# A gated graph network: the turn of h between layers, by TensorE or by VectorE and an exchange through DRAM

## The chip, the cores and the metric

The kernel runs on one core of one Trainium2 chip. The metric is device time in microseconds (us) of one execution. The engines in the text: TensorE (PE; its weight loads are PEld), VectorE (DVE), ScalarE (ACT), GpSimd (POOL) and SyncE (SP), which here only issues DMAs. Every engine works through its own list of instructions in order and waits on semaphores where it needs another's result.

## The reference

There are 16 batches of 1024 nodes with 128 features. Layer 0 is a gated graph network of four steps behind a layer norm, layer 1 a graph convolution of four steps with a batch norm over all batches. Cut to what matters:

```python
h = relu(layernorm(x))                       # per batch: (1024, 128)
for i in range(4):                           # layer 0: GRU
    m = adj.T @ (h @ weight[i])              # adj: 1024 x 1024 of 0 and 1
    r = sigmoid(m @ w_ir + h @ w_hr + b)
    z = sigmoid(m @ w_iz + h @ w_hz + b)
    n = tanh(m @ w_in + b + r * (h @ w_hn + b))
    h = (1 - z) * n + z * h
x = x + h
h = relu(layernorm(x))
for i in range(4):                           # layer 1: conv
    h = relu(adj @ (h @ W[i]) + b[i])
    h = batchnorm over all batches and nodes
return x + h
```

## The kernel before

**Two parts.** The first part (`with ExitStack() as st`) runs layer 0 for the 16 batches, in pairs; it takes two thirds of the time. The second part runs the four convolutions over all batches, from a transposed copy of the adjacency that the first part has left in DRAM (`adjT_d`). A slower path for other inputs is not taken.

**How h lies.** The gates work on `hT`, features on partitions, 1024 nodes along the free axis, in two halves of 512. The aggregation `adj.T @ h` needs h with *nodes* on partitions, as the stationary operand. So h has to be turned once per layer. `features_times(None, ...)` (L491) does it: eight 128x128 transposes on TensorE into PSUM (L498, `hw_g<-ident,h`), then for each half a copy by ScalarE that rounds to the short float type (L502, `ghw`, the high part) and a subtraction by VectorE that keeps the rest (L503, the low part). High and low are multiplied with the adjacency one after the other (L525): 32 matmuls of 128x512 per layer and batch. The weight `weight[i]` is folded into the input weights (`w_mT`), so nothing stands between turn and aggregation.

**Two streams.** `sa` takes the even batches, `sb` the odd ones, half a layer apart. `half_step(one, two)` is the unit: `one` turns h and aggregates (`split_step`, `agg_step(0)`, `agg_step(1)`), `two` runs the gates of its layer for both halves (`gate_step(0)`, `gate_step(1)`: six fp32 matmuls each, L841; sigmoid of r L853, two VectorE operations L854 and L855, tanh L858, sigmoid of z L859, and the new h L864 to L866). On TensorE the order is turn, gates, aggregation. `agg_step` ends with two copies of PSUM by ScalarE (`m`, L816), which the next half-step's gates read. The first pair's opening runs under an order written out by hand for all engines; after it only POOL and SP keep the order of the code, and a scheduler places the instructions of TensorE, VectorE and ScalarE. `behind(x)` tells it to place the following instructions after `x` on their engine.

**Work beside it.** Around the change of batches the half-steps carry more. `fetch` loads four rows of blocks of the next adjacency into `stage`, `first_four` and `last_four` round them to `row` on POOL (L578), and `glance` reads their low half-words on ScalarE (L587, `junk`, which sets a flag for inexact inputs). `ahead` loads the next x (L540) and normalizes it (`prepare`: square root L628, eight L640). `finish` exchanges input and output across the turn: VectorE transposes 32x32 blocks (L677), SP stores them to DRAM (L591) and loads them back with the blocks permuted (L598, four loads for each half). `end_step` runs the stages of a finished batch: `arrive`, `tail_norm` (L696, statistics L624), and `rest` (norm, store). `transpose_on`, in the half-step in which a stream is at layer 1, casts all eight row blocks to bf16 on POOL (L609, `half`, two buffers), has SP turn each by a DMA transpose (L610), and stores the 2 MB tile (L916). That tile shares its buffer (`turned_tile`, one buffer) with `stage`.

**Queues.** SP issues the loads of the adjacency, the exchanges and the DMA transposes, in the order of the code; POOL issues the stores of x, y and adjT and the loads of x, between its casts.

Of the kernel before, what the change touches and what calls it, by code (L numbers as in the profile page):

```python
# [341 lines left out]
def exact_path(  # L342
# [39 lines left out]
    def tmp(name):  # L382
        return ps_t.tile([P, HALF], F32, tag="tmp", name=name)

    adjT_d = [dram.tile([P, NB, N], BF16, tag=f"adjT{b}", name=f"adjT_d{b}") for b in range(B)]
    xmid_d = [dram.tile([N, C], F32, tag=f"xmid{b}", name=f"xmid_d{b}") for b in range(B)]
    ymid_d = [dram.tile([P, N], F32, tag=f"ymid{b}", name=f"ymid_d{b}") for b in range(B)]

# [145 lines left out]
    with ExitStack() as st:  # L534
# [71 lines left out]
        def transpose_rows(b, row, j, adjT):  # L606

            t = work.tile([P, N], BF16, tag="half1", name=f"half{b}_{j}", bufs=2)
            nc.gpsimd.tensor_copy(t, row.bitcast(F32))  # L609
            nc.sync.dma_start_transpose(adjT[:, :, j * P : (j + 1) * P], t)  # L610

        def norm(xt, y, name):

# [57 lines left out]

        def blocks_out(src, name):

            ds = []
            for hf in range(NH):
                t = half_tile(f"t_{name}_{hf}").bitcast(F32)
                last = nc.vector.transpose(by_nodes(t), four_ways(src[:, hf * HALF : (hf + 1) * HALF]))  # L677
                ds.append(exchange_out(t, f"{name}_{hf}"))
            return ds, last

        def tail_norm(b, xt, hT, parts=None):

            for hf in range(NH):
                if parts:
                    pt = by_nodes(parts[hf])
                else:
                    pt = tmp(f"pt_x{b}_{hf}")
                    for q in range(BH):
                        k = hf * BH + q
                        nc.tensor.transpose(pt[:, q * P : (q + 1) * P], hT[:, k * P : (k + 1) * P], ident)  # L690
                    pt = four_ways(pt)
                for q in range(BH):
                    k = hf * BH + q
                    xk = xt[:, k, :].rearrange("p (a c) -> p a c", a=4)
                    mask = maskT[:, b * NB + k : b * NB + k + 1]
                    nc.vector.scalar_tensor_tensor(xk, pt[:, q, :, :], mask, xk, ALU.mult, ALU.add)  # L696
            nt = norm_stats(xt, f"mid{b}")
            if b + 1 < B:
                y = work.tile([P, N], F32, tag="h", name=f"y_mid{b}", bufs=7)
            else:  # L700
                y = xt.rearrange("p k c -> p (k c)")
            nc.gpsimd.dma_start(xmid_d[b].rearrange("(k p) c -> p k c", p=P), xt)

            def rest():
                norm_apply(xt, y, nt)
                nc.gpsimd.dma_start(ymid_d[b], y)

            return rest

# [9 lines left out]
        class Stream:  # L719


            def __init__(self, first):
                self.b, self.i, self.tag = first, 0, "AB"[first % 2]
                self.opened, self.across, self.ends, self.stage = None, False, [], None

            def open(self, xt):

# [25 lines left out]
            def normed(self, ks):  # L753
                norm_blocks(self.xt, self.y, self.norm, ks)

            def prepare(self):
                self.next_y = work.tile([P, N], F32, tag=f"y{self.tag}", name=f"y_in{self.b + 2}", bufs=1)
                norm_apply(self.next_x, self.next_y, self.next_norm)

            def fetch(self):  # L760

                if self.i == 3 and self.b + 2 < B:
                    stage = turned_tile(f"stage{self.b + 2}").bitcast(F32)
                    self.stage = [stage[:, 2 * q : 2 * q + 2, :].rearrange("p a n -> p (a n)") for q in range(4)]
                    stage_rows(self.b + 2, self.stage, range(4))

            def first_four(self):
                if self.stage:
# [5 lines left out]
            def last_four(self):  # L774
                if self.stage:
                    self.rows += round_rows(self.b + 2, self.stage, range(4, NB))
                    with behind(self.last_act):
                        glance(self.b + 2, self.stage, range(4, NB))
                    self.stage = None

            def take(self):
                self.xt, self.y = self.next_x, self.next_y
                self.across = True
                self.hT = work.tile([P, N], F32, tag="h", name=f"h_in{self.b}", bufs=7)
                return blocks_out(self.y, f"in{self.b}")[0]

            def split_step(self):
                nm = f"{self.b}_{self.i}"
                self.hw = hw_tiles(self.b, f"ghw{nm}")
                for g in range(NH):  # L790
                    if self.i > 0:
                        features_times(None, self.hT, self.hw, g, f"g{nm}")
                        continue
                    self.split_high(g)
                    self.split_low(g)
# [12 lines left out]
            def agg_rows(self, js):  # L808
# [3 lines left out]
                if js[-1] == NB - 1:  # L812
                    self.m = []
                    for hf in range(NH):
                        m = work.tile([P, HALF], F32, tag="m", name=f"m{self.b}_{self.i}_{hf}", bufs=4)
                        nc.scalar.copy(m, self.pm[hf])  # L816
                        self.m.append(m)

            def open_gates(self):
# [4 lines left out]
                hin = self.hT[:, :HALF]  # L824
                nc.tensor.matmul(self.opened[2], w_hhT[:, 0, 2 * C : 3 * C], hin, start=True, stop=True)

            def gate_step(self, hf, between=None):
                i, nm = self.i, f"{self.b}_{self.i}_{hf}"
                if hf == 0 and not self.opened:
                    self.new = work.tile([P, N], F32, tag="h", name=f"h{nm}", bufs=7)  # L830
# [21 lines left out]
                z = work.tile([P, HALF], F32, tag="z", name=f"z{nm}")  # L852
                self.first_act = nc.scalar.activation(r, pr, AF.Sigmoid, bias=brz[:, 3 * i : 3 * i + 1])  # L853
                nc.vector.scalar_tensor_tensor(r, phn, b_hn(i), r, ALU.add, ALU.mult)  # L854
                nc.vector.tensor_add(r, pxn, r)  # L855
                if between:
                    between()
                nc.scalar.activation(r, r, AF.Tanh, bias=b_in(i))  # L858
                self.last_act = nc.scalar.activation(z, pz, AF.Sigmoid, bias=brz[:, 3 * i + 1 : 3 * i + 2])  # L859
                ho = self.new[:, cols]  # L860
                if across:
                    nc.vector.tensor_sub(four_ways(ho), hin, four_ways(r))
                else:
                    nc.vector.tensor_sub(ho, hin, r)  # L864
                nc.vector.tensor_mul(ho, ho, z)  # L865
                self.last_dve = nc.vector.tensor_add(ho, ho, r)  # L866
                if hf == NH - 1:
# [3 lines left out]
            def ahead(self):  # L871

                if self.b + 2 >= B:
                    return
                if self.i == 2 and self is sa:
                    for stream in (sa, sb):
                        stream.next_x = load_x(stream.b + 2, nc.gpsimd)
                if self.i == 3:
                    with behind(self.last_act, self.last_dve):
                        self.prepare()  # L880

            def finish(self):

# [6 lines left out]
                    self.ends = [tail_norm(*args)]  # L890
                    return
                h_in = self.hT
                outs, last = blocks_out(args[-1], f"out{args[0]}")
                parts = [half_tile(f"n_{args[0]}_{hf}").bitcast(F32) for hf in range(NH)]

                def arrive():
                    for hf in range(NH):
                        exchange_in(ins[hf], h_in[:, hf * HALF : (hf + 1) * HALF])
                    for hf in range(NH):
                        exchange_in(outs[hf], parts[hf])  # L900
                    self.ends.append(lambda: self.ends.append(tail_norm(*args, parts)))

                self.ends = [arrive]

            def end_step(self, *after):
                if self.ends:
                    with behind(*after):
                        self.ends.pop(0)()

            def transpose_on(self):  # L910

                if self.i == 1:
                    adjT = turned_tile(f"adjT{self.b}")
                    for j in range(NB):
                        transpose_rows(self.b, self.rows[j], j, adjT)
                    nc.gpsimd.dma_start(adjT_d[self.b], adjT)  # L916

            def sums_ahead(self, two):

                if self.i == 2 and self.b + 2 < B:  # L920
                    self.next_norm = norm_tiles(f"in{self.b + 2}")
                    with behind(two.last_dve):
                        norm_sums(self.next_x, self.next_norm, range(NB))

        def half_step(one, two, gated=None, halfway=None):

            if one.i > 0:
                one.split_step()
            two.gate_step(0)
            two.first_four()  # L930
            two.gate_step(1)
            two.last_four()
            if gated:
                gated()
            if one.i == 0:
                one.split_step()
            one.agg_step(0)
            if halfway:
                halfway()
            one.end_step(two.last_act)  # L940
            two.end_step(two.last_dve)
            two.ahead()
            one.transpose_on()
            one.sums_ahead(two)
            one.agg_step(1)
            two.finish()
            one.fetch()
# [118 lines left out]
        with tc.manual_schedule(engines={mybir.EngineType.Pool, mybir.EngineType.SP}):  # L1066
            written[0] = False
            for s in range(2, B // 2 * L):
                half_step(sa, sb)
                half_step(sb, sa)  # L1070
            sb.gate_step(0)
            sb.gate_step(1)
            with tc.issue_after(sb.last_act.ins):
# [16 lines left out]
    def load_adjT(b, i):  # L1090
        ts = []
        block = None if b % 2 else turned_tile(f"block{b}_{i}")
        for j in range(NB):
            t = half_tile(f"packed{b}_{i}_{j}") if b % 2 else block[:, j, :]
            nc.sync.dma_start(t, adjT_d[b][:, j, :])
            r = row_tile(f"wide{b}_{i}_{j}")
            if j % 3 == 1:
                nc.scalar.copy(r, t)  # L1098
# [269 lines left out]
```

## Time and profile before

| what | value |
|---|---|
| median of 3 runs | 1826.63 us (1825.93 to 1826.99) |
| the profiled execution | 1827.16 us |
| its span, first to last instruction | 1825.0 us |
| granted TensorE clock, mean | 0.998 |
| busy: PE / DVE / ACT / POOL | 1800.1 / 1163.1 / 1139.4 / 364.1 us |
| turns on TensorE (L498, hw_g) | 384 transposes, 50.1 us busy |
| aggregation, first part (L525, pm) | 2048 matmuls, 504.5 us busy |
| casts to bf16 (L609) / DMA transposes (L610) | 128 / 128 |
| HBM read / written | 243.35 / 73.40 MB |

How to read the lines in this document: a group has line, engine, operation, output<-input by the program's names, partitions x elements, count | busy us, mean ns of one | idle time of its engine just before, and what ended it. Matmuls overlap, so the mean of one is longer than the distance to the next. A line of waits has who waited <- for whom: us in total, times, longest. A line of the chain or the timeline has start, length, what.

### The profile page before, as it was taken

How to read it: one execution, taken by the hardware profiler on the slowest of the kernel's cores; microseconds unless marked ns; L12 is line 12 of the kernel's file. 1: busy time of each engine (PE TensorE's matmuls, PEld its weight loads, DVE VectorE, ACT ScalarE, POOL GpSimd, SP SyncE). 2: the span in 40 equal slices, each digit the busy share in tenths (PEclk: the TensorE clock that was granted, in tenths of full speed). 3: DMA queues.
4: the chain of work that ended last, by engine and by line, in shares of the span. 5: the costliest groups of instructions: out<-in, count | busy, mean ns of one | idle time of the engine just before them, and what ended most of it. 6: DMA issues, size and time to landing. Idle time of an engine off the chain costs nothing.

```text
span 1825.0 us, 22200 instructions
## 1 busy us (share of the span) xinstructions
PE 1800.1 (99%) x7102; PEld 1228.8 (67%) x7102; DVE 1163.1 (64%) x2189; ACT 1139.4 (62%) x1773; POOL 364.1 (20%) x378
## 2 busy tenths in 40 slices
PE   8999999999999999999999999999999999999997
PEld 5565665666565656565656556667778888888886
DVE  7665755666656666666566565676666666667665
ACT  5448557557556655755754755467777768768764
POOL 3223223142232232222314213110100000000010
PEclk9999999999999999999999999999999999999999
DMA  7546475375464645647537557478966666667666
GB/s 249 132 129 198 101 202 193 107 165 186 152 167 145 218 125 164 215 91 208 188 105 160 205 167 189 134 250 309 309 215 228 234 230 232 231 230 237 236 231 243
DMA packets 293020, 351.88 MB, mean 193 GB/s; under 512 B 152620, under 2 KB 187216, under 8 KB 290848
## 3 DMA queue, kind: packets, MB, share of 16 engines
q1 hardware_dynamic: 278288, 275.33, 50.5%
q0 software_dynamic: 14080, 74.80, 11.8%
q8 instruction: 57, 0.93, 0.2%
q14 instruction: 67, 0.55, 0.1%
q10 hardware_dynamic: 528, 0.26, 0.0%
HBM read 243.35 MB, written 73.40 MB: 174 GB/s over the span
## 4 chain that ended last, share of the span: by engine, by line
PE 76%; ACT 9%; DMA 6%; DVE 5%; issue 2%; SPq 1%; POOL 0%; DVEq 0%; ACTq 0%; POOLq 0%
PE pm L525 17%; PE pc_m L525 12%; PE g_z L841 9%; PE g_r L841 8%; PE pc_g_r L525 6%; PE pc_g_z L525 6%; DMA stage<-in_adj_dram 5%; PE hw_c L500 4%; PE g_hn L841 4%; PE g_xn L841 4%; ACT junk L587 3%; PE hw_g L498 2%; ACT y_in L640 1%; DVE h L865 1%; ACT z L859 1%
## 5 line engine op out<-in xcount | busy, mean ns | idle before, releaser
L525 PE MATMUL pm<-row,ghw 128*128 128x512 f32 x2048 | 504.5, 403 | 0.4 <-POOL row L564 0.3
L525 PEld LDWEIGHTS pm<-row,ghw 128*128 128x128 f32 x2048 | 384.1, 188 | 108.7 <-issue 30.9
L525 PE MATMUL pc_m<-wide,chw 128*128 128x512 f32 x1024 | 246.0, 395 | 0.0
L525 PEld LDWEIGHTS pc_m<-wide,chw 128*128 128x128 f32 x1024 | 190.5, 188 | 42.2 <-issue 4.3
L858 ACT ACTIVATE r<-r,vecs 128x512 f32<-128x512 f32 x128 | 92.0, 719 | 181.8 <-DVE r L855 181.7
L525 PE MATMUL pc_g_r<-wide,chw 128*128 128x512 f32 x464 | 187.0, 403 | 0.3 <-ACT chw L502 0.3
L578 POOL CAST row<-stage 128x1024 fp32r<-128x1024 f32 x112 | 130.8, 1179 | 273.8 <-DMA stage<-in_adj_dram 157.7
L609 POOL CAST half<-row 128x1024 bf16<-128x1024 f32 x128 | 142.2, 1127 | 209.7 <-DMA adjT<-half 196.2
L525 PE MATMUL pc_g_z<-wide,chw 128*128 128x512 f32 x464 | 180.9, 390 | 0.0
L854 DVE SCALAR_TENSOR_TENSOR r<-g_hn,vecs,r 128x512 f32<-128x512 f32 x128 | 95.5, 746 | 98.6 <-PE g_hn L841 64.9
L1100 DVE CAST wide<-block 128x1024 fp32r<-128x1024 bf16 x160 | 110.1, 693 | 74.6 <-PE pc_m L525 40.1
L1100 DVE CAST wide<-packed 128x1024 fp32r<-128x1024 bf16 x160 | 110.3, 691 | 73.3 <-PE pc_g_z L525 54.1
L864 DVE TENSOR_TENSOR h<-h,r 128x512 f32<-128x512 f32 x96 | 79.0, 823 | 112.1 <-ACT r L858 112.0
L816 ACT COPY m<-pm 128x512 f32<-128x512 f32 x128 | 68.3, 585 | 113.6 <-PE pm L525 113.6
L1098 ACT CAST wide<-packed 128x1024 fp32r<-128x1024 bf16 x96 | 100.6, 1048 | 59.3 <-PE pc_m L525 32.6
L841 PE MATMUL g_r<-m,w_mT 128*128 128x512 f32 x256 | 132.9, 601 | 4.1 <-ACT m L816 3.8
L1098 ACT CAST wide<-block 128x1024 fp32r<-128x1024 bf16 x96 | 100.7, 1049 | 56.2 <-PE pc_g_z L525 27.7
L859 ACT ACTIVATE z<-g_z,brz 128x512 f32<-128x512 f32 x128 | 86.8, 678 | 71.3 <-PE g_z L841 71.3
L841 PE MATMUL g_z<-m,w_mT 128*128 128x512 f32 x256 | 130.7, 592 | 0.0
L841 PE MATMUL g_xn<-m,w_mT 128*128 128x512 f32 x256 | 130.7, 592 | 0.0
L503 DVE TENSOR_TENSOR ghw<-hw_g,ghw 128x512 fp32r<-128x512 f32 x96 | 62.1, 687 | 104.0 <-ACT ghw L502 103.9
L587 ACT ACTIVATE junk<-stage 128x1024 bf16<-128x1024 uint16 x112 | 117.8, 1052 | 16.2 <-DMA stage<-in_adj_dram 14.4
(182 smaller groups left out, 2804.2 us busy)
## 6 DMA issues: line engine op xcount, KB each, us to landing
packed<-adjT_d SPq DMA_DIRECT2D x256, 256.0 KB, 6.3
block<-adjT_d SPq DMA_DIRECT2D x256, 256.0 KB, 5.2
stage<-in_adj_dram SPq DMA_DIRECT2D x120, 512.0 KB, 5.1
adjT_d<-adjT POOLq DMA_DIRECT2D x16, 2048.0 KB, 7.0
xmid_d<-x POOLq DMA_DIRECT2D x16, 512.0 KB, 5.2
y<-ymid_d POOLq DMA_DIRECT2D x16, 512.0 KB, 5.7
ymid_d<-y_mid POOLq DMA_DIRECT2D x15, 512.0 KB, 3.1
x<-in_x_dram POOLq DMA_DIRECT2D x14, 512.0 KB, 11.0
```

The lines of the kernel that those rows point to most:

```text
L500: nc.tensor.matmul(pt[:, q * P : (q + 1) * P], src, w, start=True, stop=True)
L525: nc.tensor.matmul(pm[hf], hw[s][:, j * P : (j + 1) * P], rows[j][:, hf * HALF : (hf + 1) * HALF], start=(j == 0 and s == 0), stop=(j == N ...
L578: nc.gpsimd.tensor_copy(t, stage[j % 4])
L587: nc.scalar.activation(junk, lows, AF.Copy, accum_out=low[:, k : k + 1])
L609: nc.gpsimd.tensor_copy(t, row.bitcast(F32))
L841: nc.tensor.matmul(po, wT[:, i, g * C : (g + 1) * C], rhs, start=start, stop=stop)
L854: nc.vector.scalar_tensor_tensor(r, phn, b_hn(i), r, ALU.add, ALU.mult)
L858: nc.scalar.activation(r, r, AF.Tanh, bias=b_in(i))
L859: self.last_act = nc.scalar.activation(z, pz, AF.Sigmoid, bias=brz[:, 3 * i + 1 : 3 * i + 2])
L864: nc.vector.tensor_sub(ho, hin, r)
L1098: nc.scalar.copy(r, t)
L1100: nc.vector.tensor_copy(r, t)
```

## The change

The turn of h goes from TensorE to VectorE and DRAM in five of the six turns of a pair. After each half of the gates, VectorE transposes the new h in 32x32 blocks and SP stores it (`half_away`); at the start of the next half-step SP loads both halves back with the blocks permuted (`halves_back`); ScalarE and VectorE then make the high and the low part from SBUF (`split_back`), placed behind the first half's gates. `turned_away` keeps the odd stream's turn before layer 3, and all turns of the opening, on TensorE. The casts and DMA transposes of the adjacency become a generator (`transposes`) that `feed.some` advances by one or two at four places of a half-step, for both batches of a pair one after the other, with the store at the beginning of the half-step after the last transpose. Stores of x and y, loads of the next x and the loads of the boundary exchange are collected in `later` and issued at the beginning of the next half-step (`deliver`). The square root and scale of the next norm move to between the two halves of the gates (`root_ahead`), four of the eight reads of low half-words go to VectorE (`look`), and the parts of a finished batch come back into the old h instead of a half tile. `adjT_d` is laid out block by block.

```diff
-    adjT_d = [dram.tile([P, NB, N], BF16, ...
+    adjT_d = [dram.tile([NB, P, N], BF16, ...
...
-            nc.sync.dma_start_transpose(adjT[:, :, j * P : (j + 1) * P], t)
+            return lambda: nc.sync.dma_start_transpose(adjT[:, :, j * P : (j + 1) * P], t)
+        def transposes(batches):
+            for b, rows in batches:
+                adjT = turned_tile(f"adjT{b}")
+                ahead = transpose_rows(b, rows[0], 0, adjT)
+                for j in range(NB):
+                    go = ahead
+                    if j + 1 < NB:
+                        ahead = transpose_rows(b, rows[j + 1], j + 1, adjT)
+                    go()
+                    yield j
+                nc.gpsimd.dma_start(adjT_d[b].rearrange("k p n -> p k n"), adjT)
...
+        def half_out(t, src, hf, name):
+            nc.vector.transpose(by_nodes(t), four_ways(src[:, hf * HALF : (hf + 1) * HALF]))
+            return exchange_out(t, f"{name}_{hf}")
...
+            def root_ahead(self):
+                if self.i == 2 and self.b + 2 < B:
+                    with behind(self.last_act):
+                        norm_root(self.next_norm, 0, NB)
+                        norm_scale(self.next_norm, 0, NB)
...
-                    with behind(self.last_act):
-                        glance(self.b + 2, self.stage, range(4, NB))
+                    with behind(self.last_dve):
+                        for j in range(4, NB):
+                            look(self.b + 2, self.stage[j % 4], j)
...
+            def turned_away(self, i):
+                return not written[0] and i < L and not (self is sb and i == 3)
+            def half_away(self, hf):
+                if self.turned_away(self.i + 1 - hf):
+                    nm = f"{self.b}_{self.i + 1 - hf}"
+                    self.outs.append(half_out(cross_tile(f"t_h{nm}_{hf}"), self.new, hf, f"h{nm}"))
+            def halves_back(self):
+                nm = f"{self.b}_{self.i}"
+                self.backs = [cross_tile(f"n_h{nm}_{hf}") for hf in range(NH)]
+                for d, t in zip(self.outs, self.backs):
+                    exchange_in(d, t)
+                self.hw = hw_tiles(self.b, f"ghw{nm}")
+            def split_back(self, g, *after):
+                if self.outs:
...
+                    with behind(*after):
+                        self.split = [
+                            nc.scalar.copy(hi, back),
+                            nc.vector.tensor_sub(lo, back, hi.bitcast(F32)),
+                        ]
...
         def half_step(one, two, gated=None, halfway=None):
+            feed.open = True
+            deliver()
+            if one is sb and one.i == 0 or not sb.started:
+                feed.jobs, sb.started = transposes([(s.b, s.rows) for s in (sa, sb)]), True
             if one.i > 0:
                 one.split_step()
+            if one.i > 0:
+                feed.some(2)
             two.gate_step(0)
+            two.half_away(0)
             two.first_four()
-            two.gate_step(1)
+            two.root_ahead()
+            one.split_back(0, two.last_act, two.last_dve)
+            one.split_back(1, two.last_act, two.last_dve)
+            if one.i > 0:
+                feed.some(1)
+            two.gate_step(1, None, one.split)
+            two.half_away(1)
+            if one.i == 0:
+                feed.some(1)
             two.last_four()
...
             one.agg_step(0)
...
-            one.end_step(two.last_act)
-            two.end_step(two.last_dve)
-            two.ahead()
-            one.transpose_on()
-            one.sums_ahead(two)
+            one.end_step(two.last_act, *one.split)
+            two.end_step(two.last_dve, *one.split)
+            with behind(*one.split):
+                two.ahead()
+            feed.some(1)
+            with behind(*one.split):
+                one.sums_ahead(two)
             one.agg_step(1)
...
-            nc.sync.dma_start(t, adjT_d[b][:, j, :])
+            nc.sync.dma_start(t, adjT_d[b][j])
```

In the changed program `split_back` stands at lines 852 (ScalarE's copy) and 853 (VectorE's subtraction), the VectorE transpose at 704.

## The prediction

> **What bounds the kernel now.** I read the busy shares on the page first, then the waits of TensorE, the chain that ended last in order of time, the groups, and the landing times of the exchange.
>
> ```profile
> PE 1800.1 (99%) x7102; PEld 1228.8 (67%) x7102; DVE 1163.1 (64%) x2189; ACT 1139.4 (62%) x1773; POOL 364.1 (20%) x378
> ```
> ```profile
> PE g_r L841 <- ACT m L816: 3.8, 14, 0.6
> ...
> PE g_z L841 <- ACT z L859: 0.9, 3, 0.4
> ```
> TensorE is idle for 25 us of 1825 and hardly ever waits. So what is taken off TensorE counts in full, and every wait that is put in front of it counts in full too. One half-step of the recurrent part, from the chain in order of time (start, length, what):
>
> ```profile
> 323.14 1.95 PE g_r L841 x4
> 325.09 0.86 PE g_hn L841 x2
> 325.95 0.86 PE g_xn L841 x2
> 326.81 1.72 PE g_z L841 x4
> 328.52 1.72 PE g_r L841 x4
> 330.24 0.86 PE g_hn L841 x2
> 331.10 0.86 PE g_xn L841 x2
> 331.96 1.72 PE g_z L841 x4
> 333.67 7.29 PE pm L525 x32
> 340.96 0.87 PE hw_g L498 x8
> ```
> Set 0 at the first gate matmul (323.14). g_z of the first half is complete at 5.38, that of the second at 10.53. The timeline of TensorE lets the first aggregation matmul begin at 333.11, so at 9.97, and the next half-step begin at 17.8; with a turn it is 0.87 more. From one aggregation's start to the next it is 18.46 (333.11 to 351.57) with a turn, 17.59 without.
>
> ```profile
> L498 PE MATMUL hw_g<-ident,h 128*128 128x128 f32 x384 | 50.1, 272 | 0.2 <-ACT w_mT L488 0.2
> L864 DVE TENSOR_TENSOR h<-h,r 128x512 f32<-128x512 f32 x96 | 79.0, 823 | 112.1 <-ACT r L858 112.0
> L502 ACT CAST ghw<-hw_g 128x512 fp32r<-128x512 f32 x96 | 52.2, 600 | 1.0 <-PE hw_g L498 1.0
> L503 DVE TENSOR_TENSOR ghw<-hw_g,ghw 128x512 fp32r<-128x512 f32 x96 | 62.1, 687 | 104.0 <-ACT ghw L502 103.9
> L803 DVE TENSOR_TENSOR ghw<-y_in,ghw 128x512 fp32r<-128x512 f32 x30 | 21.0, 699 | 47.9 <-ACT ghw L799 47.9
> ```
>
> **Names.** A pair of batches takes eight half-steps A0, B0, A1, B1, A2, B2, A3, B3: stream A (even) or B aggregates, at layer 0 to 3, while the other stream's gates run. A turn stands in six of them, and the exchange replaces five: A1, B1, A2, B2, A3. B3 keeps its turn.
>
> **What is removed.** The order of the changed program's instructions on TensorE holds 11 turns of 48: eight B3 and three in the first pair, which runs under the hand-written order. 37 are gone. TensorE issues the eight transposes in 0.87 us, so 37 x 0.87 = 32.2 us. The Trainium skill ("VectorE: DVE Perf Modes", The three transpose paths) has 390 ns for a TensorE transpose of 128x128 in bf16; that would be an estimate of 296 x 0.39 = 115 us; the row (0.87/8 = 0.11 us) decides. The PSUM evictions (L502, L503) become the same two operations on SBUF, same size: priced alike.
>
> **The exchange itself, beside other work.** Per turn: two VectorE transposes (t_out L677 has a median of 0.69 us), two stores, eight loads. Nearest rows (the batch-boundary exchange): stores land in 2.0 to 6.4 us, median 4.7 (cross_in<-t_in) and 2.8 (cross_out<-t_out); 64 KB loads in about 2.0 to 2.8, and eight of them leave SP in 3.76 us. The new h's second half is ready on VectorE at about 16 of its half-step; store 2 to 5, loads 3.8 + 2: the data is there at about 5 to 8 of the next half-step. ScalarE can begin the copy (call it HI, line 852) after z of the first half, at 5.38 + 0.7 = 6.1, and TensorE wants it at 9.97. That is the cover: 2 to 5 us. It costs nothing while it holds; past it, each us is a us of TensorE.
>
> **Where the new order makes TensorE wait.** Here HI and the subtraction behind it (LO, line 853) are placed among the gates' instructions of the in-order engines, and the built order says where.
> - A1: ScalarE has sigmoid r, z, tanh, sigmoid r, z, HI, HI. HI is behind the *second* z, which needs the last gate matmul (10.53). 10.6 + 0.63 (z) + 0.60 (HI) = 11.85, against 9.97: 1.9 us. VectorE's LO ends 0.7 later, at 12.6, while the two matmuls on HI give 0.5 of cover: 0.3 more. Sum 2.2.
> - B1: HI is behind the first z, so it ends by 6.7. But tanh follows HI (to 7.2), and VectorE has subtract, g_hn's operation of the second half, multiply, add, add, LO: six at 0.62 to 0.69, to 11.2, against 9.97 + 0.49 = 10.46: 0.8 to 0.9.
> - A2: the same with five: to 10.8, 0.4 to 0.5.
> - B2, A3: LO stands ahead of those; 0.
> Together 3.6 us a pair, and 7 pairs: 25 us. This is the half of the sum that I am least sure of; its bounds are 15 (VectorE's separate slots of 0.61 in the timeline hide B1 and A2, only A1's stays) and 39 (next part but one).
>
> **Stalls that can go.** From 296.82 (aggregation of B3) to 444.30 a pair takes 147.48, and 6 x 18.46 + 2 x 17.59 = 145.94: 1.5 us are lost, in B3, A0 and B0, where the reads of the low half-words (junk L587, 1.24 with its accumulator read) hold z and m on ScalarE. The change moves half of them to VectorE behind the last h (4 x 1.21 = 4.8 us; VectorE's 16 to 20 of the half-step, so its first operation in A0 goes from 3 to about 4.5, still ahead of TensorE's next need at 6.9). Between 0 and 1.5 x 7 = 11: I take 5, since the other half stays in the same place.
>
> **Parts with one answer.** Casts and DMA transposes one at a time (128 before and after), later stores of x and y, and the 2 KB pieces of the adjacency's store move work of POOL and SP that TensorE does not wait for while the cover above holds. What is queued behind them is SP: a DMA transpose issues in 1.23 us and lands in 3.0 to 8.5, and the exchange's stores now stand behind it. The square-root table load moves between the two gate halves of B2 and A3 (1.28 twice): sigmoid r of the second half starts at 10 to 11 instead of 7; the next user of that bank comes at 17.8. The second part of the kernel reads the same bytes and never waited for them: 0.
>
> **A rule that speaks against it.** L503 reads one operand from PSUM; its 96 runs lie within 680 to 693 ns. L864 reads two from SBUF: median 693, mean 823, up to 1793, and the long ones lie beside POOL's casts (402.2, 408.0). LO now reads two from SBUF, and the casts are spread over five half-steps. If a cast meets one VectorE operation ahead of each gating LO, it is 0.65 x 3 x 7 = 14 us: the upper bound, 39. L803, with two SBUF operands, has a mean of 699, so I leave it out of the centre. The Trainium skill ("GPSIMD Engine Reference", Specifications) says that GpSimd shares its SBUF interface with VectorE, in contention with two SBUF inputs; by it the sum would take these 14 in.
>
> **Sum.** The profiled execution took 1827.16 (span 1825.0 and 2.2 around it), 0.5 above the median 1826.63. 1827.2 - 32.2 + 25 - 5 = 1815.
>
> **Rivals.**
> - *Full gain*: TensorE's stalls stay under a quarter of what I count. 1827 - 32 + 6 - 5 = 1796 to 1803. For it: the in-order sums use whole latencies. Against: A1's does not depend on them. 0.11.
> - *Break-even*: the contention of the rule comes in: 1815 + 14 = 1829; within the 0.2% (3.7 us) that a measurement of this kernel can tell from no change. 0.11.
> - *SP is late (slower)*: in A2 the first transpose of B's adjacency waits for the 2 MB store of A's, which POOL now issues behind the y store and two x loads; before, those 3.5 MB took 14.0 us (381.36 to 395.4). SP stands still until then, with h's stores behind it: transposes 1.25 each, the cast for the third 3.2 + 1.1 after the first, loads at about 4.5 of B2 and data at 10.5: past the need. Where transposes land in 5 rather than 3.2 us, the other four follow. One us late in all five is 5 x 7 = 35: 1850. It decides from data later than about 9 us after the first gate matmul. For it: SP is one queue, and transposes take the DMA engines whole (shares of 0.9 in slices of that window). Against: in the other four half-steps 2 to 5 us of cover. 0.33.
> - *It does not do what it says*: excluded, the turns are gone from the program.
> The forecast's own case has 0.45, from 1803 to 1823.
>
> **Range and chances.** 1798 leaves out most of the full gain, 1846 the worst of SP's lateness, about 1 in 10 at each end. Faster 0.45 + 0.11 = 0.56, same 0.11, slower 0.33.
>
> **What would show it.** Right: hw_g with 88 instructions; in the timeline of A1 the aggregation starts at about 12 after the first gate matmul, with TensorE waiting for ScalarE's L852 by about 2 us, seven times; B1 and A2 waiting for L853 by 0.5 to 0.9; B2 and A3 not at all. Wrong: waits of L852 for DMA n_h ahead of TensorE's (SP's rival); pairs of 142 us (full gain); TensorE's waits at L841 for m or z of more than 2 us a pair, which I count at nothing.

## The result, and the profile after

The changed kernel takes 1826.38 us (median of 12 runs, 1822.72 to 1830.26); the kernel before took 1826.64 beside it (12 runs). The ratio is 1.0000, 95% interval 0.9992 to 1.0008: no change that can be measured. 1815 was forecast, so 11 us of the forecast gain are missing. The profiled execution took 1826.22 us (span 1824.3, granted clock 0.995).

The busy shares and the waits of TensorE:

```profile
PE 1772.9 (97%) x6806; PEld 1202.5 (66%) x6806; DVE 1249.3 (68%) x2319; ACT 1076.2 (59%) x1661; POOL 364.4 (20%) x378
```
```profile
PE pm L525 <- DVE ghw L853: 15.5, 7, 3.2
PE g_r L916 <- ACT m L891: 9.4, 8, 1.9
PE hw_g L498 <- DVE h L943: 4.2, 5, 1.7
PE g_z L916 <- ACT z L935: 3.1, 4, 1.0
```
TensorE has 27 us less to do and stands idle for 51 us instead of 25: the turns went, and waits took their place one for one. The groups that answer to those shown of before:

```profile
L941 DVE TENSOR_TENSOR h<-h,r 128x512 f32<-128x512 f32 x96 | 75.3, 785 | 69.7 <-ACT r L934 69.6
L853 DVE TENSOR_TENSOR ghw<-n_h,ghw 128x512 fp32r<-128x512 f32 x74 | 57.4, 783 | 23.0 <-ACT ghw L852 22.2
L852 ACT CAST ghw<-n_h 128x512 fp32r<-128x512 f32 x74 | 44.4, 611 | 43.8 <-DMA n_h<-cross_h 43.8
L498 PE MATMUL hw_g<-ident,h 128*128 128x128 f32 x88 | 12.8, 276 | 4.4 <-DVE h L943 4.2 <-ACT w_mT L488 0.2
```
Two things are new: L852 waits 43.8 us for the exchanged data, and TensorE's turn in B3 waits for h.

**Where, half-step by half-step.** The timeline of TensorE gives the start of every aggregation. This table is worked out from it: the mean distance, over seven pairs of one execution (six for B3), from the start of the named aggregation to the next one's. A column holds the named aggregation and the gates up to the next: the gates of half-step A1 stand in column B0, those of B1 in column A1. 17.59 is a half-step without a turn, 18.46 one before a turn on TensorE. TensorE can move gate matmuls from one half-step into the one before, so B0 and A1 are added together; the expectations call this sum "A1 and B1 together".

| kernel | A0 | B0+A1 | B1 | A2 | B2 | A3 | B3 | pair |
|---|---|---|---|---|---|---|---|---|
| before | 17.92 | 36.92 | 18.60 | 18.46 | 18.45 | 18.85 | 18.37 | 147.6 |
| after | 17.59 | 36.52 | 17.60 | 20.77 | 17.58 | 19.43 | 18.42 | 147.9 |
| without a stall, after | 17.59 | 35.18 | 17.59 | 17.59 | 17.59 | 18.46 | 17.59 | 141.6 |

So each pair loses 1.34 in B0+A1 (felt at B1's first gates), 3.18 in A2, 0.97 in A3 (B3's turn comes late) and 0.83 in B3 (about what experiment 1 has there without any exchange).

**A2, the largest.** Timelines of ScalarE, VectorE and TensorE (start, length; in brackets the idle time before and who ended it):

```profile
233.68 0.61 ACT L852 CAST ghw<-n_h 128x512 fp32r<-128x512 f32 x1
234.19 0.72 ACT L934 ACTIVATE r<-r,vecs 128x512 f32<-128x512 f32 x1
238.63 0.62 ACT L852 CAST ghw<-n_h 128x512 fp32r<-128x512 f32 x1 [3.72 <-DMA n_h<-cross_h]
239.16 0.68 ACT L928 ACTIVATE r<-g_r,brz 128x512 f32<-128x512 f32 x1
```
```profile
239.87 0.75 DVE L929 SCALAR_TENSOR_TENSOR r<-g_hn,vecs,r 128x512 f32<-128x512 f32 x1 [3.51 <-ACT r L928]
240.54 0.68 DVE L943 TENSOR_TENSOR h<-h,r 128x512 f32<-128x512 f32 x1
241.14 0.69 DVE L853 TENSOR_TENSOR ghw<-n_h,ghw 128x512 fp32r<-128x512 f32 x1
```
```profile
237.65 1.03 PE L525 MATMUL pm<-row,ghw 128*128 128x512 f32 x2
241.88 8.72 PE L525 MATMUL pm<-row,ghw 128*128 128x512 f32 x30 [3.21 <-DVE ghw L853]
```
The *second* half of h is late; TensorE would need it only half an aggregation (7.29 / 2 = 3.6 us) after 237.65. But ScalarE stands at it with sigmoid r of the other stream behind, VectorE stands at L929 for that sigmoid, and behind L929 waits the low part of the *first* half, which ScalarE had read by 234.3. That is what TensorE waits for. In all seven pairs its wait is 2.2 us more than the time from the aggregation's start to that of the second L852 (-1.7 to 1.0 us, waits of 0.5 to 3.2), so how late the data lands sets the stall. B1 of the same kernel shows the other order: there the second L852 waits for the DMA too (0.7 to 2.1 us in six of seven pairs), but sigmoid r stands ahead of it, and B1 takes 17.60. Why the data is late, on the queues of GpSimd and SP:

```profile
227.72 0.56 POOL L735 DMA_DIRECT2D ymid_d<-y_mid  x1 [12.84 <-ACT y_mid L667]
228.27 1.78 POOL L540 DMA_DIRECT2D x<-in_x_dram  x2
230.04 0.89 POOL L623 DMA_DIRECT2D adjT_d<-adjT  x1
```
```profile
226.06 4.13 SPq L598 DMA_DIRECT2D n_h<-cross_h  x8
242.89 2.62 SPq L610 DMA_TRANSPOSE adjT<-half  x2
245.60 0.53 SPq L591 DMA_DIRECT2D cross_h<-t_h  x1
```
SP issues the eight loads in time, by 230.2, while GpSimd sends off 3.5 MB. In this stretch a load of 64 KB takes up to 8.8 us to land; over the kernel the median is 2.1. SP itself then stands until 242.89, when the 2 MB are stored, as the rival "SP is late" had it; h's stores behind it still reach B2 in time (L852 waits for no DMA there).

**And the clock.** The stretches of the pause, of the first matmuls behind it, and of the rest of A2 (length, busy times, then the granted clock):

```profile
237.65:241.88 4.23, 1.02 (x5) 0.35 (x3) 2.01 (x4) 1.78 (x3) 0.00 (x0) 1.00 0.84 344
241.88:245.40 3.52, 3.52 (x9) 2.74 (x10) 2.69 (x5) 0.72 (x1) 0.00 (x0) 0.54 0.42 82
245.40:250.43 5.03, 5.03 (x23) 4.14 (x22) 3.88 (x19) 0.03 (x1) 2.21 (x2) 0.99 0.80 193
```
After the 3.2 us pause the granted clock is 0.54 for 3.5 us, which costs about 1.6 more (0.46 of 3.5). It happens in A2 of three of the seven pairs.

### The profile page after: what moved, and what is told of

The parts are those of the page before. It is cut to its first block, busy times and chain, and to the rows that moved or that the text cites. A ratio compares the mean times of both kernels' runs of the same rounds, so it can differ in the third digit from the quotient of the medians.

```text
span 1824.3 us, 22144 instructions
## 1 busy us (share of the span) xinstructions
PE 1772.9 (97%) x6806; PEld 1202.5 (66%) x6806; DVE 1249.3 (68%) x2319; ACT 1076.2 (59%) x1661; POOL 364.4 (20%) x378
## 4 chain that ended last, share of the span: by engine, by line
PE 63%; DVE 13%; DMA 9%; ACT 7%; SPq 4%; issue 4%; POOL 0%; DVEq 0%; ACTq 0%; POOLq 0%
PE pm L525 13%; PE pc_m L525 12%; PE g_r L916 6%; PE pc_g_r L525 6%; PE pc_g_z L525 6%; PE g_z L916 6%; PE hw_c L500 4%; DMA n_h<-cross_h 4%; PE g_xn L916 3%; SPq L598 3%; DVE h L943 2%; PE g_hn L916 2%; DVE low L604 2%; DVE h L942 2%; DMA cross_out<-t_out 1%
## 5 line engine op out<-in xcount | busy, mean ns | idle before, releaser
L525 PE MATMUL pm<-row,ghw 128*128 128x512 f32 x2048 | 514.9, 407 | 15.5 <-DVE ghw L853 15.5
L929 DVE SCALAR_TENSOR_TENSOR r<-g_hn,vecs,r 128x512 f32<-128x512 f32 x128 | 95.3, 745 | 180.0 <-ACT r L928 103.2
L609 POOL CAST half<-row 128x1024 bf16<-128x1024 f32 x128 | 138.3, 1090 | 311.0 <-DMA adjT<-half 296.8
L941 DVE TENSOR_TENSOR h<-h,r 128x512 f32<-128x512 f32 x96 | 75.3, 785 | 69.7 <-ACT r L934 69.6
L1239 DVE BATCH_NORM_STATS2 stats<-feat 128x6 f32<-128x512 f32 x128 | 84.1, 686 | 46.9 <-ACT feat L1238 45.8
L928 ACT ACTIVATE r<-g_r,brz 128x512 f32<-128x512 f32 x128 | 87.8, 686 | 43.7 <-PE g_r L916 43.3
```

Of the source, the lines that this page charges most:

```text
L525: nc.tensor.matmul(pm[hf], hw[s][:, j * P : (j + 1) * P], rows[j][:, hf * HALF : (hf + 1) * HALF], start=(j == 0 and s == 0), stop=(j == N ...
L1239: nc.vector.bn_stats(stats[:, b * NH + hf, :], dst)
```

## Experiments

Times are medians; the ratio is to the kernel before, measured beside it (1825.8 to 1826.6).

**1. The change without the exchange (turns_on_pe).**

```diff
-                return not written[0] and i < L and not (self is sb and i == 3)
+                return False
```


> All turns of h go back to TensorE (48 turns); everything else of the change stays: transposes fed one at a time, later stores, half of the low-half-word reads on VectorE. If the parts without the exchange cost nothing, as the prediction has it: between the kernel before and 5 us under it, 1822 to 1827, hw_g with 384 instructions, half-step A2 (start of its aggregation to that of B2's) at 18.46 like the others. If the one-at-a-time feed or the delivery at the beginning of the half-step costs something by itself (SP's and POOL's new order), 1830 or more, with TensorE waiting at g_r for m or at hw_g for h.

1820.21 us, ratio 0.9965 (0.9953 to 0.9977): 6.3 us faster than before. Its half-steps are all 18.46 and 17.59 but for B3 (18.40). So the parts beside the exchange gain 6 us (columns A0, B1 and A3 no longer lose time, column B3 still does; which part does it was not separated), and the exchange *loses* 6.2 (1826.4 against 1820.2). With 32.2 us of turns taken away, its waits cost 38.4. The table has the same: 1.34 + 3.18 + 0.97 = 5.5 a pair, 38 in seven.

**2. Fewer exchanges (a2_on_pe, three_away).** `turned_away` leaves out A2's turn, or A2's and A3's.

> The exchange stays in A1, B1, B2 and A3; only the turn in A2 goes back to TensorE. If the missing gain is A2's stall (22.2 us over seven pairs by the distances of the aggregations), 0.87 of turn comes back and 3.2 of stall goes in each pair: (3.2 - 0.87) x 7 = 16 us less, 1810. If each exchange costs about what it saves, or the late data only finds the next half-step, the time stays within 4 us of the changed kernel, 1822 to 1830.

1813.73, 0.9929 (0.9916 to 0.9943). A2's distance is 17.58, and 12.7 us of the 16 expected arrive: A3's grew from 19.43 to 20.80. There TensorE's waits for h at the turn rose from 4.2 to 9.8 us:

```profile
PE hw_g L498 <- DVE h L943: 9.8, 6, 2.9
```
In A3 too, the second L852 waits for the DMA (2.0 to 4.5 us in this trace) with sigmoid r behind it; here this makes the new h late.

> The exchange only in A1, B1 and B2; A2 and A3 have their turns on TensorE. Against the run with A2 on TensorE (1813.7): A3 pays 0.87 a pair for its turn, and the distance from A3's to B3's aggregation, 20.8 on the mean there (TensorE waits for h at B3's turn since ScalarE's sigmoid r stands behind the late data of A3), falls to 18.5: (2.3 - 0.87) x 7 = 10 us less, 1803. If B3's wait has another cause (B's transposes on SP, the square roots between the gates), 1814 to 1820.

1809.55, 0.9908 (0.9893 to 0.9922). A3's distance is 18.46, so B3's wait did come from A3's exchange; 4 us of the 10 expected arrived in the median (the profiled execution of a2_on_pe, 1818, was slower than its median, so its 20.80 overstates).

**3. The burst held back (burst_held).** In A2, in place of `feed.some(2)` at the start (`kept` holds the y store, which `deliver` would have issued there):

```diff
+            if held:
+                one.split_back(0, two.last_act, two.last_dve)
+                one.split_back(1, two.last_act, two.last_dve)
+                tick = small.tile([P, 1], F32, tag="tick", ...)
+                nc.gpsimd.tensor_copy(tick, one.hw[0][:, N - 1 :].bitcast(F32))
+                for go in kept:
+                    go()
+                feed.some(2)
```


> In A2 GpSimd holds back the y store and the 2 MB store of the adjacency (2.5 of the 3.5 MB that it issues there) until ScalarE has made the high part of the second half of h, by a one-column copy that reads it. Contention theory: the second half of h lands 4 us sooner, ScalarE's L852 waits for no DMA in A2, A2's distance falls from 20.8 to at most 18.4: 17 us less; L852 moves behind the second z in B2 in this build, which gives back up to 1.3 x 7 = 9 us: 1809 to 1820. SP theory (what hurts is that SP stands at the first transpose of the next adjacency): that transpose waits as long or longer, h's stores behind it are later, and B2's aggregation is late by 2 us or more: 1826 to 1840.

1817.78, 0.9951 (0.9937 to 0.9964). In A2 of the third pair (515 to 540) the loads' landing times were, in the changed kernel and here:

```profile
DMA to landing us min/median/max: 1.9/2.7/8.6
```
```profile
DMA to landing us min/median/max: 1.9/2.2/5.0
```
The second L852 then waits 0.3 us at most in A2, where it had waited 1.0 to 3.7. That GpSimd's burst makes the data late is shown; SP's longer stand (7.1 us into the aggregation instead of 5.2) cost B2 nothing. Yet A2's distance is 21.6, not the 18.4 at most that was expected: 1.7 of it are gates of the next half-step pulled ahead (B2 has 15.9), and about 2.1 a new loss. VectorE and GpSimd of this run, in the same A2:

```profile
533.83 0.74 DVE L929 SCALAR_TENSOR_TENSOR r<-g_hn,vecs,r 128x512 f32<-128x512 f32 x1
534.49 2.81 DVE L943 TENSOR_TENSOR h<-h,r 128x512 f32<-128x512 f32 x1
537.22 1.28 DVE L853 TENSOR_TENSOR ghw<-n_h,ghw 128x512 fp32r<-128x512 f32 x2
```
```profile
533.26 0.57 POOL L735 DMA_DIRECT2D ymid_d<-y_mid  x1
533.82 0.90 POOL L623 DMA_DIRECT2D adjT_d<-adjT  x1
534.72 2.02 POOL L609 CAST half<-row 128x1024 bf16<-128x1024 f32 x2
```
Two casts (2.02 us) met an addition of two SBUF operands, which took 2.81 instead of 0.69: the whole length of both casts was added. The Trainium skill ("SBUF — State Buffer", SBUF: two separate sides) calls the port pair that the two engines share an exclusive lock, not a split, with VectorE in it when both its inputs are in SBUF. The length agrees, and by and large so does its rule that the operation that starts first keeps the pair: in this trace none of the 51 additions, subtractions and products of two SBUF operands that start ahead of a cast, with no DMA being issued on GpSimd, takes over 0.8 us, and 83 of the 86 that start while one runs do. The addition shown starts 0.23 us ahead of the first cast, but while GpSimd is still issuing the 2 MB store; it ends 0.56 us after the second cast. The same happens in A2 of five pairs; in the other two the first low part (2.96) or several operations (1.2 to 1.5) are lengthened. From when GpSimd holds the port there does not show in the records.

**4. The order (late_order, sig_first).** late_order puts the first half's parts ahead of the second gates, and the second half's behind them:

```diff
-            one.split_back(0, two.last_act, two.last_dve)
-            one.split_back(1, two.last_act, two.last_dve)
+            one.split_back(0, two.last_act, two.mid_dve)
...
             two.gate_step(1, None, one.split)
+            one.split_back(1, two.last_act, two.last_dve)
...
-                self.first_act = nc.scalar.activation(r, pr, AF.Sigmoid, ...)
-                nc.vector.scalar_tensor_tensor(r, phn, b_hn(i), r, ALU.add, ALU.mult)
+                with behind(*after[:1]):
+                    self.first_act = nc.scalar.activation(r, pr, AF.Sigmoid, ...)
+                with behind(*after[1:]):
+                    nc.vector.scalar_tensor_tensor(r, phn, b_hn(i), r, ALU.add, ALU.mult)
```
(z, too, is placed behind `after[:1]`.)

> Same exchange, same queues; only the order on ScalarE and VectorE is changed: the high part of the first half (L852) ahead of the second sigmoid r and z, the low part (L853) ahead of the second g_hn operation, and both parts of the second half behind all gates of the second half. Order theory (late data costs only because the gates of the other stream stand behind it in order): the distance of A2 falls from 20.8 to about 18, A1 and B1 together from 36.5 to 35.5, B3 by 0.4: about 4 us a pair, 28 us in seven pairs, 1798 to 1803, although the second half lands as late as before. Contention theory (the data itself is what TensorE waits for): at most A1's 1 us a pair, 1817 to 1826.

1847.28, 1.0117 (1.0101 to 1.0132): a clear miss. A2 fell to 17.73 as expected, but B0+A1 rose to 37.6, B2 to 19.3 and A3 to 22.6. The waits moved:

```profile
PE pm L525 <- DVE ghw L853: 24.3, 20, 3.5
PE hw_g L498 <- DVE h L945: 13.4, 7, 2.3
```
```profile
411.62 4.65 PE L525 MATMUL pm<-row,ghw 128*128 128x512 f32 x18
419.53 3.48 PE L525 MATMUL pm<-row,ghw 128*128 128x512 f32 x14 [1.55 <-DVE ghw L853]
```
Eighteen of the 20 waits for L853 stand in front of the nineteenth matmul of an aggregation (in A1, B2 and A3), as in the two lines: there TensorE needs the low part of the *second* half, and behind all gates that comes too late. In B2 the first half is late as well (L852 waits 0.4 to 2.1 us for the DMA in six of seven pairs, with the gates' sigmoids behind it), and the new h with it. So the run shows that the second half can also stand too far back; it does not speak against the order as the cause in A2.

sig_first changes only what the reading of A2 blames: the place of the second half.

```diff
-            one.split_back(1, two.last_act, two.last_dve)
...
-            two.gate_step(1, None, one.split)
+            two.gate_step(1, lambda: one.split_back(1, two.first_act, two.mid_dve), one.split)
```


> Only the place of the second half's parts moves: its high part (L852) behind the sigmoid r of the gates' second half, its low part (L853) behind the second half's add; the first half as in the changed kernel. In A2 sigmoid r no longer stands behind the late data, so VectorE's g_hn operation, the end of the first half's h and the first low part follow at once: A2's distance from 20.8 to about 18.2, and A3's (to the aggregation of B3) from 19.4 to about 18.7. Order theory: 3.3 x 7 = 23 us, 1803. If a stall that goes in A2 comes back in B2 (late_order: 19.7 there instead of 17.6, because GpSimd's 2 MB store still holds SP, with h's stores behind it, until the same moment), about 2 of the 3.3 return: 1817.

1805.27, 0.9893 (0.9878 to 0.9907), 21 us faster than the changed kernel. ScalarE in the A2 shown above, and TensorE:

```profile
233.62 0.61 ACT L852 CAST ghw<-n_h 128x512 fp32r<-128x512 f32 x1
234.13 0.72 ACT L934 ACTIVATE r<-r,vecs 128x512 f32<-128x512 f32 x1
234.81 0.69 ACT L928 ACTIVATE r<-g_r,brz 128x512 f32<-128x512 f32 x1
237.50 0.62 ACT L852 CAST ghw<-n_h 128x512 fp32r<-128x512 f32 x1 [2.00 <-DMA n_h<-cross_h]
```
```profile
237.59 7.87 PE L525 MATMUL pm<-row,ghw 128*128 128x512 f32 x32
```
The data is as late as before (the second L852 in A2 waits for it in six of seven pairs, up to 3.5 us), and TensorE hardly feels it: A2 17.77, A3 18.82; only B0+A1 rose, from 36.5 to 37.5. Lateness came from the DMA; the loss came from what stood behind it.

**5. A1 and B1 (z_behind_high, four_away, sig_a1_on_pe, sig_a1_on_pe2, sig_root_a1).** z_behind_high moves the second z under the `with behind(*after[:1])` of tanh.

> One line: the sigmoid z of the gates' second half is placed behind the high part of the second half (L852), as tanh is already. In A1 the data is there early (L852 never waits for a DMA there), so both high parts end 3 us sooner and TensorE need not pull three pairs of the next half-step's gate matmuls ahead; B1's wait for m at its first gate (0.8 to 1.9) goes: 1.0 x 7 = 7 us, 1819. If TensorE's filling hides A1's lateness wholly and the wait for m stays, or the later z makes the next turn's data later by as much: 1825 to 1828.

1828.68, 1.0016 (1.0005 to 1.0027), a miss: in A1 the first L852 moves 2.5 us ahead, but the second then does wait for the DMA (1.0 to 2.0 us, 3.5 in one pair), TensorE still pulls two pairs of gates ahead, m waits as before, and B0+A1 stays (36.41); and in A2, for a reason not traced, the second L852 waits longer for the DMA (up to 4.5 us; 21.69). four_away joins it to sig_first's edit, with A2 on TensorE.

> The exchange in A1, B1, B2 and A3 (A2 on TensorE), the second half's parts placed as in the run before (high part behind sigmoid r, low part behind the add), and z behind the first high part. If order is what turns late data into loss, B3's 20.8 falls to 18.6 (16 us) and A1's and B1's 36.3 to 35.4 (6 us): 1813.7 - 22 = 1792. If only one of the two holds, 1798 to 1808; if neither, 1814.

1810.50, 0.9917 (0.9904 to 0.9930): A3 falls to 18.71 by the order, B0+A1 rises to 37.04. Only the order half held, and the time is a little above the range given for that. sig_a1_on_pe is sig_first with A1's turn on TensorE.

> Like sig_first, with A1's turn back on TensorE (exchange in B1, A2, B2, A3). A1 and B1 together take 37.3 in sig_first; with the turn and no late part they would take 36.1: 1.2 x 7 = 9 us less, 1797, if A1's exchange costs more than its turn. If the wait for m comes from y_mid alone and not from the exchange, 0.87 x 7 = 6 us more, 1811.

1823.65, 0.9986 (0.9973 to 0.9998), outside both expectations: A2's distance went back to 20.15. In this build the scheduler put the finished batch's square root and two table loads between z and tanh in B1, and A2's first half came 4 us late. sig_a1_on_pe2 keeps that root behind tanh (`one.end_step(two.last_act, two.tanh, *one.split)`).

> Like sig_a1_on_pe (A1's turn on TensorE, 1823.7), but in B1 the square root of the finished batch stays behind tanh of the second half; in that run the scheduler had put it with two table loads ahead of tanh, and A2's first half of h landed 4 us late. Theory (h half a step later on ScalarE is data later in the next half-step): A2's distance falls from 20.1 to about 17.7, 2.4 x 7 = 17 us, 1807; A1 and B1 together then take 36.1 to 37.0 against 37.3 in sig_first. If A2's lateness there came from A1's turn on TensorE itself, it stays at 1820 or more.

1804.31, 0.9877 (0.9860 to 0.9895): A2 17.65, and L852 waits for no DMA there. So 3 us of ScalarE ahead of one tanh in each pair cost 19 us in all, a half-step further on. B0+A1 is 36.8 with A1's turn on TensorE, 37.5 without: in this order A1's exchange earns nothing. sig_root_a1 keeps the exchange and the root behind tanh, and takes the root and scale of the finished even batch ahead:

```diff
             two.root_ahead()
+            if one is sa and one.i == 1 and one.ends:
+                with behind(two.last_act):
+                    one.ends[0].root()
```


> Like sig_first (1805.3), but in A1 the square root and scale of the finished even batch stand between the gates' two halves (as the next input's already do in B2 and A3), so that its eight L667 find their scale (L663) ready and end before TensorE's aggregation; the stores on GpSimd keep their places. If m at B1's first gate waits because ScalarE's m stands behind L667, and L667 behind VectorE's late L663: TensorE's 12.6 us of waits for m fall to about 4, A1 and B1 together from 37.3 to 36.1, 8 us less, 1797. If the wait belongs to A1's late high part alone: 1804 to 1807.

1803.66, 0.9874 (0.9857 to 0.9890): the lowest median, with sig_first and sig_a1_on_pe2 within 2 us of it, not told apart, and 23 us under both the kernel before and the changed one. TensorE's waits for m, in sig_first and here:

```profile
PE g_r L916 <- ACT m L891: 12.6, 8, 2.3
```
```profile
PE g_r L924 <- ACT m L899: 5.6, 9, 1.8
```
B0+A1 falls from 37.5 to 36.6: m did stand behind L667. But B1 gives back 0.4 and A3 0.3, and in the median 1.6 of the 8 us arrive.

**6. SP (sig_b2_late_y).** Meant to free m by moving L667 a half-step later:

> Like sig_first (1805.3), and the eight operations that normalize a finished batch (L667, y_mid) run a half-step later than their square root and scale, behind the second z; in B2 sigmoid r and z of the second half stand behind the first high part, as they did in sig_first. In sig_first ScalarE's m in A1 stands behind L667, which waits for VectorE's scale (L663): TensorE waits for m at B1's first gate by 12.6 us in all. Theory m (that queue is the cause): the wait goes, A1 and B1 together from 37.3 to 35.5, 1.8 x 7 = 12 us less, 1793. Rival (m waits because TensorE pulled gates ahead of A1's aggregation, since L852 stands behind the second z): the wait stays, 1803 to 1807.

1874.96, 1.0259 (1.0245 to 1.0273). B0+A1 fell to 36.2 as theory m has it, and A2 rose to 27.0. GpSimd and SP:

```profile
242.76 0.89 POOL L540 DMA_DIRECT2D x<-in_x_dram  x1 [15.09 <-DVE st_in L651]
243.64 0.89 POOL L623 DMA_DIRECT2D adjT_d<-adjT  x1
```
```profile
252.68 2.62 SPq L610 DMA_TRANSPOSE adjT<-half  x2
255.39 0.53 SPq L591 DMA_DIRECT2D cross_h<-t_h  x1
```
The load of x was held up for 15 us (0.3 us after the last L667 of the odd batch, which reads the x of before and now ends at 242.46, it goes out; that L667 releases it is read from this, the view names L651), the 2 MB store behind it on GpSimd, B's first transpose behind that store on SP, and h's stores behind the transpose: B2's aggregation waited 10.6 us for L852. This is the prediction's rival, with 10 us more of it: SP standing until 242.9 costs nothing; until 252.7 it costs 10 us a pair (1875.0 - 1805.3 over seven).

## Why the prediction was wrong, step by step

- **Gross gain, 0.87 a turn: right.** 18.46 against 17.59 in turns_on_pe and in the changed kernel.
- **Stalls that go, 5 us (0 to 11): right in size.** The change without the exchange is 6.3 faster than before. The loss went in columns A3 and A0 (the gates of half-steps B3 and B0), which the prediction named, and in B1, which it did not; column B3 (half-step A0), the largest of the three that it named, still loses 0.8. That the moved reads of low half-words did it is not shown.
- **"Where the new order makes TensorE wait", 3.6 a pair, 25 us: the step that failed.** It measured 5.5 a pair, 38 us. A1's aggregation does start 12.5 after the first gate matmul (204.00 - 191.53), for the reason given. But TensorE fills the hole with six gate matmuls of the next half-step, and what remains is B1's wait for m, which the prediction counted at nothing: 1.3 for A1 and B1 together instead of 3.0. A2 was put at 0.4 to 0.5 and took 3.2, of which 0.7 is the lower clock (1.6 in three of seven); A3's effect on B3 was put at 0 and took 1.0. Over seven pairs that is 12 us less than counted in A1 and B1, and 19 and 7 more in A2 and A3.
- **The term behind it: "the data is there at about 5 to 8 ... That is the cover: 2 to 5 us".** In A2 ScalarE gets the second half from 1.7 us before the aggregation's start to 1.0 after it, on the prediction's scale (aggregation at 9.97) at 8 to 11. The landing time was taken from the medians of the boundary exchange's loads (2.0 and 2.8) and not from loads beside 3.5 MB; the burst in A2 was seen and used only for SP's stand. And the cover was weighed against TensorE's need alone. The second half was not late for TensorE; it was late for ScalarE's next instruction.
- **The rivals.** The time came out near where break-even had it, at 1829, but not for its reason. SP's mechanism is real (experiment 6), in the place that was named, but in this change it stays short of its point; the 14 us of the port rule do not show in the changed kernel's A2, and lengthening by casts shows as about 2.1 us in burst_held, where they fall on the gating operations. The waits of L852 for DMA n_h, named as the sign of SP's rival, came in A2 from GpSimd's traffic; in B1 and A3 their cause was not tested.
- With the measured terms (38.4 by the table, 5.49 x 7) the prediction's own sum closes: 1827.2 - 32.2 + 38.4 - 6.3 = 1827.1, against 1826.4.

What remains open: why the data of A2 lands at such different times from pair to pair, why the clock falls behind some of the waits and not behind others, and why the changed kernel's times vary by 7 us between runs.

## What to carry to other kernels

When a value comes back from a DMA into an in-order engine, ask first what stands behind the copy that reads it, on that engine and on the next; put the part that is needed last behind work that others wait for, but no further back than its own need allows. One such move of the second half was worth 21 us here, while holding back the traffic that made it late was worth 9 and a stricter order lost 21. Price a load by loads that ran beside the same traffic, and count the lower clock that a pause of TensorE leaves behind.

## What the runs showed of the hardware that was not expected

- The lower clock behind a pause of TensorE (0.50 for about 3.4 us, some 1.6 us lost) followed waits of 3.21, 2.64 and 1.88 us in A2 of three pairs, and not those of 3.12 and 2.46 in two others. The Trainium skill ("TensorE: Matmul & The Clock Gate", What's actually happening) has free-running windows of 3.4 us, one idle one of which halves the clock. The depth and the length of the slow stretch agree, and free-running windows fit a pause whose length does not decide alone; that a whole window has to be idle does not fit the 1.88, and the measurement decides.
- VectorE's operations with an operand in PSUM do not lengthen beside GpSimd's casts here, those with two in SBUF do. In burst_held 32 of the 128 executions of L930 (one operand in PSUM) overlap a cast, and none takes over 693 ns. Of L943 (two in SBUF) 44 do, with a median of 1407; the other 84 stay under 695. Over all of them (minimum, median, maximum in ns):

```profile
L930 DVE TENSOR_TENSOR r<-g_xn,r x128: 643/691/693, 26.8 to 1196.2; 128x512 f32<-128x512 f32 x128
L943 DVE TENSOR_TENSOR h<-h,r x128: 662/692/2814, 32.7 to 1199.7; 128x512 f32<-128x512 f32 x128
```
